# A multi-query attention and expert kernel: w1's turned blocks by way of DRAM, the last batch's rows turned by VectorE, Wq loaded between rows B and C

## The chip, the cores and the metric

One core of a Trainium2 chip runs the whole program. The metric is the device time of one execution in microseconds (us), the median over the runs. Beside it there is one profiled execution, taken by the hardware profiler, with a record of each instruction and its waits.

## The reference

For 8 batches of 1024 rows of 128 numbers, all in float32 (cut to what matters):

```python
xn = layernorm(x)                                  # x: (8, 1024, 128)
Q = einsum('bnd,hdk->bhnk', xn, proj_q)            # 8 query heads
K = einsum('bmd,dk->bmk', xn, proj_k)              # one key head
V = einsum('bmd,dv->bmv', xn, proj_v)              # one value head
weights = softmax(einsum('bhnk,bmk->bhnm', Q, K), axis=-1)
O = einsum('bhnm,bmv->bhnv', weights, V)
Y = einsum('bhnv,hdv->bnd', O, proj_o)
mid = einsum('amh,ehn->aemn', xn, w1)              # w1: (8, 128, 512)
ffn = einsum('aemn,enh->amh', mid, w2)             # w2: (8, 512, 128)
return x + Y + ffn
```

The expert part has no nonlinearity, so it is one 128 x 128 matrix, the sum over experts of w1 times w2. In the same way query and key weights are multiplied together per head (`wqk`), and value and output weights (`wvo`).

## The kernel before

**Tiles.** The unit of work is a score tile i: 128 queries of one head u = i // 8 against the 1024 keys of its batch; there are 8 batches x 8 heads x 8 = 512 tiles (`NS`). For each tile TensorE makes the scores in one of two PSUM slots of 1024 columns (`logits`, tile `pl`: 8 matmuls), VectorE takes the row maxima (`nmax`), ScalarE the exponents and their sums (`e`, two buffers) and scales them by the reciprocal (`divide`). VectorE turns the weights in 32 x 32 blocks (`weights_t`, tile `turned`, two buffers of four tiles each), and after every fourth tile SP issues 16 DMAs of 128 KB, each from 32 partitions to 32, that bring the blocks to their places (`move_blocks`, into `g0` for the first half of a head, `g1` for the second). GpSimd forms sums and differences of halves of these (`sum_early`, `sums_late`: 4.56 us each), and TensorE multiplies them with combinations of the values (`product`) with seven products instead of eight, into four PSUM banks `acc0` to `acc3` that are kept for a whole batch. These products run 12 tiles (`LAG`) behind the scores.

**Order.** The schedule is written by hand: each engine does its instructions in the order of the program, and the loop `for i in range(NS)` at the end of the kernel states it. A DMA that SP issues waits in SP's order for what it reads, and holds all behind it. The first tiles carry, beside the scores, a list `early[i]` of weight preparations. `bank(name)` gives these the four banks `acc0` to `acc3` in turn, before the products need them.

**The start.** The rows of batch 0 (`x_0`) come in four pieces of two chunks each, called A to D here, 128 KB each, on SP's queue; `wk` and Wq (`wq`: head 0 first, then the other seven heads, 448 KB) come on ScalarE's queue, then wv, wo, w1 (2 MB) and w2 on SP's. VectorE makes moments and normalized rows of each pair of chunks (`stats_pair`, `norm_pair`), TensorE transposes them (`xn_t_pair`). `keep_clock` multiplies zeros, so that TensorE is not idle. `wq_part` transposes Wq's heads through a bank and ScalarE copies them out; `wqk_product` multiplies them with the key weights.

**w1 and w2.** The product wants w1 with its middle dimension on the partitions. `turn_w1(k)`, in tiles 0 to 3, has VectorE turn a quarter of w1 in blocks of 32 x 32, into `w1_turned`; in tile 3, after `load_rows(1)` (rows of batch 1, 512 KB), `move_w1` moves the blocks back into the buffer `w1s` with 16 DMAs of 128 KB, 32 partitions to 32. `ffn_weights(k)` multiplies with w2, 32 matmuls in each of tiles 8 to 11, into the bank `pwf` (`acc3`), and the result `wfT`, which lies in the buffer of the value weights `s_v`, is transposed to `wf` in tile 12.

**Rows of later batches.** For batch b > 0 the rows are loaded ahead, normalized by GpSimd, turned by VectorE in blocks (`turn_rows`, tile `xnt`) and moved by 16 DMAs of 32 KB in runs of 1 KB, four each at four tiles (`move_rows`), into `xnT`. The columns of `xnT` are then in the order of these blocks. The last batch is different: it needs the natural order, and `xn_t` has TensorE transpose its eight chunks into a score slot, from which ScalarE copies them.

Of the kernel before, what the change touches and what calls it, by code (L numbers as in the profile page):

```python
# [17 lines left out]
def kernel(  # L18
# [42 lines left out]
    nc = tc.nc  # L61
# [24 lines left out]
    rows = ctx.enter_context(tc.tile_pool(name="rows", bufs=3))  # L86
    work = ctx.enter_context(tc.tile_pool(name="work", bufs=2))
    small = ctx.enter_context(tc.tile_pool(name="small", bufs=4))
    ps_sc = ctx.enter_context(tc.tile_pool(name="ps_sc", bufs=2, space=PSUM))
    ps_acc = ctx.enter_context(tc.tile_pool(name="ps_acc", bufs=1, space=PSUM))  # L90

# [3 lines left out]
    def slot(name):  # L95
        return ps_sc.tile([P, S], F32, tag="sc", name=name)
# [7 lines left out]

    def bank(name):

        banks[0] = (banks[0] + 1) % (3 if pwf else 4)
        return ps_acc.tile([P, GS], F32, tag=f"acc{banks[0]}", name=name)


# [50 lines left out]
    x_0 = late.tile([P, NB, D], F32, tag="x", name="x_0")  # L161
    for i in range(GN):
        nc.sync.dma_start(x_0[:, ts(i, 2)], chunked(x[0])[:, ts(i, 2)])
    nc.scalar.dma_start(wq[:, 1:], proj_q[1:].rearrange("h d k -> d h k"))
    nc.sync.dma_start(wv, proj_v)
    nc.sync.dma_start(wo, proj_o.rearrange("h d v -> d h v"))
    nc.sync.dma_start(w1s.rearrange("p (e n) -> p e n", e=NE), w1.rearrange("e h n -> h e n"))
# [21 lines left out]
    wqk = const.tile([P, H, P], F32, tag="wqk", name="wqk")  # L189
    wvo = const.tile([P, H, P], F32, tag="wvo", name="wvo")  # L190
    wf = const.tile([P, P], F32, tag="wf", name="wf")
    spread = const.tile([P, 3 * HP], F32, tag="spread", name="spread")
    moments = const.tile([P, B, NB, 2], F32, tag="moments", name="moments")
    rstd = const.tile([P, B, NB], F32, tag="rstd", name="rstd")
# [3 lines left out]
    def transposed(dst, srcs, name, copy):  # L198

        pt = blocks(bank(name))  # L200
        for c, src in enumerate(srcs):
            nc.tensor.transpose(pt[:, c, :], src, ident)  # L202
        copy(dst, pt[:, : len(srcs), :])
# [12 lines left out]
        both_halves(pt, wvT, woT[:, ts(g, GN), :])  # L216
        nc.scalar.copy(wvo[:, ts(g, GN), :], blocks(pt))

    wfT = s_v[:, :P]
    w1T = w1s.rearrange("p (r i a) -> p r i a", r=NQ, a=Q)  # L220

    def turn_w1(k):

        i = ts(k, NB)
        nc.vector.transpose(
            w1_turned.rearrange("p (k i a) -> p i k a", k=NQ, a=Q)[:, i],
            w1s.rearrange("p (i k q) -> p i k q", k=NQ, q=Q)[:, i],
        )

    def move_w1():  # L230
        n = NE * NFC * Q
        for r in range(NQ):
            for k in range(NQ):
                nc.sync.dma_start(w1s[ts(k, Q), ts(r, n)], w1_turned[ts(r, Q), ts(k, n)])  # L234

    def ffn_weights(k):
        if k == 0:
            pwf.append(ps_acc.tile([P, GS], F32, tag="acc3", name="pwf"))
        n = NE * NFC
        for i in range(8 * k, 8 * k + 8):  # L240
            w2_i = w2s[2 * i // n][:, i % (n // 2)]
            both_halves(pwf[0][:, :P], w2_i, w1T[:, :, i, :], i == 0, i == n - 1)
        if k == 3:
            nc.scalar.copy(wfT, pwf.pop()[:, :P])
# [30 lines left out]
            xns.pop(b).rearrange("p c (k q) -> p c k q", q=Q),  # L275
        )

    def move_quarters(dst, src, r):

        n = S // NQ  # L280
        for k in range(NQ):
            nc.sync.dma_start(dst[ts(k, Q), ts(r, n)], src[ts(r, Q), ts(k, n)])

    def move_rows(b, r):

        if r == 0:
            xnTs[b] = batch.tile([P, S], F32, tag="xnT", name=f"xnT_{b}")
        move_quarters(xnTs[b], turned_rows[b], r)
        if r == NQ - 1:
            del turned_rows[b]  # L290

    def xn_t(b):
        xnTs[b] = batch.tile([P, S], F32, tag="xnT", name=f"xnT_{b}")
        pt = slot(f"pxn_{b}")
        for c in range(NB):
            nc.tensor.transpose(pt[:, ts(c, P)], xns[b][:, c, :], ident)
        nc.scalar.copy(xnTs[b], pt)

    def xn_t_pair(k, copy):

# [352 lines left out]
    def one(t):  # L653
        return t.rearrange("p (c x) -> p c x", c=1)

    def wq_part(first, last):
        transposed(
            wqT[:, first:last], [wq[:, h] for h in range(first, last)], f"pwq_{first}", nc.scalar.copy
        )

    def wo_part(g):
        heads = range(g * GN, (g + 1) * GN)
# [10 lines left out]
    def norm_pair(k):  # L673
        normalize(0, x_0, nc.vector, (2 * k, 2 * k + 1))

    def stats_pair(k):
# [15 lines left out]
    xn_t_pair(1, nc.scalar.copy)  # L692
    stats_pair(2)
    queries(0, 0, P)
    keep_clock(P)
    stats_pair(3)
    logits_half(0, 0)
    norm_pair(2)
    xn_t_pair(2, nc.scalar.copy)
    norm_pair(3)  # L700
    wq_part(1, 4)
    xn_t_pair(3, nc.vector.tensor_copy)
    logits_half(0, 1)
    wq_part(4, 8)
    queries(0, P, GS)
    exponents(0)

    early = {
        0: [lambda: wqk_product(1, 3), lambda: queries(0, GS, S)],
        1: [  # L710
            lambda: wqk_product(4, 4),
            lambda: queries(1, 0, GS),
# [42 lines left out]
    for i in range(NS):  # L755
        m = i % GN
        if i > 0:
            logits(i)
        for task in early.get(i, ()):
            task()  # L760
        if 0 <= i - 1 < NS - GN:
            weights_t(i - 1)
        divide(i)
        if i < 4:
            turn_w1(i)
        if i == 3:
            load_rows(1)
            move_w1()


        v, n = divmod(i - LAG, NB)
        if n == 6 and v + 1 >= 0:
            sum_early(v + 1)


        if i >= LAG:
            run((PAIRS if i < NS - GN else LAST_PAIRS)[m] + (n == 0 and v % H == H // 2 + 1) * 2)
            if n == 0:
                sums_late(v, nc.gpsimd)
        if i % NB == 0 and i > 0 and i // NB + 1 < B * H:  # L780
            queries(i // NB + 1)
        if i % NB == GN and i >= LAG:
            s, r = divmod(i + 20, 32)
            if s < 2 * B:
                values(s, r // NB)


        if i == 8:
            load_x(0)
        if i == NS // B:  # L790
# [79 lines left out]
```

## Time and profile before

| | us |
|---|---|
| median of 4 runs | 1924.18 |
| lowest and highest | 1923.86 and 1924.26 |
| the profiled execution, whole | 1924.22 |
| its span, first to last instruction | 1922.3 |

| engine | busy us of the span |
|---|---|
| TensorE (PE) | 1911.9 |
| GpSimd (POOL) | 1406.1 |
| VectorE (DVE) | 1396.5 |
| ScalarE (ACT) | 1357.8 |

TensorE's granted clock is 1.000 of full speed over the whole span. DMAs move 295 MB, 154 GB/s on average. In the lists below, PE is TensorE, PEld its weight loads, SPq a DMA issue by SP, and L103 is line 103 of the kernel; L103 is a helper that all products in two halves share, so they are told apart by the tile that they write: `pl` scores, `pq` queries, `pv` values, `pwqk`, `pwvo` and `pwf` weights. A matmul's length includes its way through the array, so successive groups overlap a little; groups of eight start every 1.72 us where nothing waits. A window line gives the window, its length, the busy time of PE, PEld, DVE, ACT and POOL with the number of instructions, the clock, the busy share of the DMA engines and what they moved in GB/s.

### The profile page before, as it was taken

Reading aid. Unit: us, or ns where it says so; the run is one execution under the profiler, and the core shown is the slowest. Engines: PE = TensorE matmul, PEld = TensorE weight load, DVE = VectorE, ACT = ScalarE, POOL = GpSimd, SP = SyncE. Lnnn points to the kernel's source line nnn. Section 1 sums busy time; section 2 is a strip of 40 time slices with the busy share of each in tenths; the row PEclk is TensorE's granted clock in tenths of the full one; section 3 lists DMA queues with packets and bytes.
Section 4 is the critical chain, followed back from the end, with each engine's and each line's share of the span. In section 5 each row is a group of like instructions: output and inputs, shape, how many; then the busy total and the mean of one; then the engine's idle time right before and its main releaser. Section 6 shows DMA issues by size and latency. Waiting matters only on the chain.

```text
span 1922.3 us, 26881 instructions
## 1 busy us (share of the span) xinstructions
PE 1911.9 (99%) x9037; PEld 664.4 (35%) x9037; DVE 1396.5 (73%) x1774; ACT 1357.8 (71%) x1829; POOL 1406.1 (73%) x593
## 2 busy tenths in 40 slices
PE   9999999999999999999999999999999999999998
PEld 4444443333333333333333333333333333333333
DVE  6767778767786777777777777776777776777775
ACT  7677777777777777777777777777777766777764
POOL 2787777788776886777967778768787676677764
PEclk9999999999999999999999999999999999999999
DMA  7776667666766766677667676676766667567673
GB/s 206 173 158 149 141 154 155 152 161 154 158 146 151 172 149 148 151 159 166 142 153 158 150 173 143 149 155 148 183 137 141 145 155 172 132 140 158 153 163 90
DMA packets 138074, 295.08 MB, mean 154 GB/s; under 512 B 36816, under 2 KB 70352, under 8 KB 137936
## 3 DMA queue, kind: packets, MB, share of 16 engines
q1 hardware_dynamic: 136192, 292.50, 67.8%
q8 instruction: 73, 1.20, 0.3%
q10 hardware_dynamic: 1744, 0.85, 0.2%
q14 instruction: 65, 0.53, 0.1%
HBM read 13.76 MB, written 4.19 MB: 9 GB/s over the span
## 4 chain that ended last, share of the span: by engine, by line
PE 96%; SPq 1%; ACT 1%; DVE 1%; DMA 0%; issue 0%; DVEq 0%
PE pl L103 45%; PE acc L460 39%; PE pq L103 6%; PE pv L103 5%; PE acc L493 1%; SPq L415 1%; SPq L234 0%; DVE nmax L359 0%; ACT e L367 0%; DMA x<-in_L_attn_x_dram 0%; ACT e L377 0%; DVE turned L399 0%; ACT scratch_vf L367 0%; PE pe L388 0%; ACT scratch_vf L377 0%
## 5 line engine op out<-in xcount | busy, mean ns | idle before, releaser
L103 PE MATMUL pl<-xnT,qT 128*64 128x512 f32 x4096 | 968.7, 593 | 2.7 <-ACT qT L317 1.5
L359 DVE TENSOR_REDUCE nmax<-pl 128x1 f32<-128x1024 f32 x512 | 625.8, 1222 | 413.7 <-PE pl L103 413.0
L460 PE MATMUL acc<-g,vf 128*64 128x512 f32 x2560 | 852.9, 592 | 0.2 <-PE pwf_t L202 0.2
L367 ACT ACTIVATE e<-pl,nmax 128x1024 f32<-128x1024 f32 x508 | 565.7, 1114 | 399.4 <-DVE nmax L359 399.4
L377 ACT ACTIVATE e<-e,rinv 128x1024 f32<-128x1024 f32 x508 | 583.6, 1149 | 118.7 <-DVE rinv L376 118.6
L399 DVE STREAM_TRANSPOSE turned<-e 128x1024 f32<-128x1024 f32 x508 | 628.3, 1237 | 14.8 <-DMA g<-turned 4.0
L103 PEld LDWEIGHTS pl<-xnT,qT 128*64 128x64 f32 x4096 | 299.5, 137 | 580.0 <-issue 529.3
L460 PE MATMUL acc<-f,vf 128*64 128x512 f32 x1016 | 487.0, 592 | 0.0
L435 POOL TENSOR_TENSOR g<-g,g 128x2048 f32<-128x2048 f32 x63 | 287.0, 4556 | 270.7 <-DMA g<-turned 145.1
L460 PEld LDWEIGHTS acc<-g,vf 128*64 128x64 f32 x2560 | 253.0, 137 | 504.6 <-issue 499.3
L430 POOL TENSOR_TENSOR f<-g 128x2048 f32<-128x2048 f32 x63 | 287.0, 4556 | 175.2 <-PE acc L460 89.8
L438 POOL TENSOR_TENSOR f<-g,g 128x2048 f32<-128x2048 f32 x63 | 287.4, 4562 | 4.9
L436 POOL TENSOR_TENSOR g<-f,g 128x2048 f32<-128x2048 f32 x63 | 287.0, 4555 | 0.0
L460 PEld LDWEIGHTS acc<-f,vf 128*64 128x64 f32 x1016 | 139.2, 137 | 0.0
L103 PE MATMUL pq<-xnT,wqk 128*64 128x512 f32 (+1 forms) x516 | 121.6, 589 | 0.0
L103 PE MATMUL pv<-wvo,xnT 128*64 128x512 f32 x512 | 120.9, 592 | 0.0
L376 DVE RECIPROCAL rinv<-sums 128x1 f32<-128x1 f32 x512 | 83.7, 164 | 48.8 <-ACT scratch_vf L367 4.3
L367 ACT ACTIVATION_READ_ACCUMULATOR e<-pl,nmax 128x1 f32 x508 | 97.2, 191 | 0.0
L337 POOL TENSOR_TENSOR vf<-vf 128x256 f32<-128x256 f32 x64 | 46.8, 732 | 28.5 <-ACT vf L336 28.5
L317 ACT COPY qT<-pq 128x1024 f32<-128x1024 f32 (+2 forms) x67 | 64.0, 955 | 0.2 <-PE pq L103 0.2
L103 PEld LDWEIGHTS pv<-wvo,xnT 128*64 128x64 f32 x512 | 37.7, 137 | 72.2 <-issue 68.5
L103 PEld LDWEIGHTS pq<-xnT,wqk 128*64 128x64 f32 x516 | 37.8, 137 | 70.3 <-issue 69.7
(111 smaller groups left out, 543.1 us busy)
## 6 DMA issues: line engine op xcount, KB each, us to landing
g<-turned SPq DMA_DIRECT2D x2032, 128.0 KB, 2.4
xn<-in_L_attn_x_dram SPq DMA_DIRECT2D x7, 512.0 KB, 4.7
out<-yt SPq DMA_DIRECT2D x112, 32.0 KB, 1.9
xnT<-xnt SPq DMA_DIRECT2D x96, 32.0 KB, 1.9
x<-in_L_attn_x_dram SPq DMA_DIRECT2D x6, 512.0 KB, 4.3
out_dram<-x SPq DMA_DIRECT2D x6, 512.0 KB, 5.3
scratch_g<-in_L_ffn_w_dram SPq DMA_DIRECT2D x1, 2048.0 KB, 11.4
scratch_g<-scratch_vf SPq DMA_DIRECT2D x16, 128.0 KB, 2.4
```

The costliest lines, as they stand in the source:

```text
L103: nc.tensor.matmul(dst[r], lhsT=lhsT[:, r], rhs=rhs, start=start, stop=stop)
L317: copy(qTs[u][:, first:last], pq[:, :n])
L359: nc.vector.reduce_max(nmax, pl, AX.X, negate=True)
L367: nc.scalar.activation(es[i], pl, AF.Exp, bias=nmax, accum_out=sums[i])
L376: nc.vector.reciprocal(rinv, sums.pop(i))
L377: nc.scalar.mul(es[i], es[i], rinv)
L399: nc.vector.transpose(turned[k].rearrange("p k c t q -> p c k t q")[:, :, :, j, :], es.pop(i).rearrange("p (c k q) -> p c k q", k=NQ, q=Q),)
L430: nc.gpsimd.tensor_add(f1s[u], key_half(g0s[u], 0), key_half(g0s[u], 1))
L435: engine.tensor_sub(x1, y1, x1)
L436: engine.tensor_sub(x2, f1s[u], y1)
L438: engine.tensor_sub(f4s[u], y2, x2)
L460: nc.tensor.matmul(accs[b, acc][ts(half, HP)], lhsT=vfs[u // GN][:, u % GN, f, c, :], rhs=w[:, :, c, :], start=(h == 0 and c == first), st ...
```

## The change

Four parts:

- The seven heads of Wq are loaded on SP's queue, between the pieces B and C of the rows. Three of them are transposed where an idle matmul stood, ahead of the first scores, the other four ahead of the second half of tile 0's scores; the copies are separate steps, and the product of heads 1 to 3 comes before the queries of tile 0's second part.
- Each turned quarter of w1 is stored in a DRAM tile as soon as VectorE has turned it; in tile 3, after the rows of batch 1, four loads of 512 KB, each to 32 partitions, bring all of it back into `w1s` in its new order.
- `ffn_weights` moves from tiles 8 to 11 to tiles 9 to 12 and from `acc3` to `acc2`; its result gets a tile of its own, and its transposition moves from tile 12 to tile 14.
- The last batch's rows are turned by VectorE and moved like those of the others, with a destination that restores the natural order: 16 DMAs of 32 KB in pieces of 128 bytes. `xn_t` is gone.

```diff
--- before.py
+++ after.py
@@ -86,6 +86,7 @@
+    dram = ctx.enter_context(tc.tile_pool(name="dram", bufs=1, space=bass.MemoryType.DRAM))
@@ -104,7 +105,8 @@
 
     def bank(name):
 
-        banks[0] = (banks[0] + 1) % (3 if pwf else 4)
+        assert not pwf
+        banks[0] = (banks[0] + 1) % 4
         return ps_acc.tile([P, GS], F32, tag=f"acc{banks[0]}", name=name)
 
 
@@ -161,7 +163,8 @@
     x_0 = late.tile([P, NB, D], F32, tag="x", name="x_0")
     for i in range(GN):
         nc.sync.dma_start(x_0[:, ts(i, 2)], chunked(x[0])[:, ts(i, 2)])
-    nc.scalar.dma_start(wq[:, 1:], proj_q[1:].rearrange("h d k -> d h k"))
+        if i == 1:
+            nc.sync.dma_start(wq[:, 1:], proj_q[1:].rearrange("h d k -> d h k"))
     nc.sync.dma_start(wv, proj_v)
     nc.sync.dma_start(wo, proj_o.rearrange("h d v -> d h v"))
     nc.sync.dma_start(w1s.rearrange("p (e n) -> p e n", e=NE), w1.rearrange("e h n -> h e n"))
@@ -189,6 +192,7 @@
     wqk = const.tile([P, H, P], F32, tag="wqk", name="wqk")
     wvo = const.tile([P, H, P], F32, tag="wvo", name="wvo")
     wf = const.tile([P, P], F32, tag="wf", name="wf")
+    wfT = const.tile([P, P], F32, tag="wfT", name="wfT")
     spread = const.tile([P, 3 * HP], F32, tag="spread", name="spread")
     moments = const.tile([P, B, NB, 2], F32, tag="moments", name="moments")
     rstd = const.tile([P, B, NB], F32, tag="rstd", name="rstd")
@@ -216,26 +220,28 @@
         both_halves(pt, wvT, woT[:, ts(g, GN), :])
         nc.scalar.copy(wvo[:, ts(g, GN), :], blocks(pt))
 
-    wfT = s_v[:, :P]
     w1T = w1s.rearrange("p (r i a) -> p r i a", r=NQ, a=Q)
 
+    w1_way = dram.tile([P, NQ, NE * NFC, Q], F32, tag="w1", name="w1_turned")
+
     def turn_w1(k):
 
         i = ts(k, NB)
+        turned_i = w1_turned.rearrange("p (k i a) -> p k i a", k=NQ, a=Q)[:, :, i]
         nc.vector.transpose(
-            w1_turned.rearrange("p (k i a) -> p i k a", k=NQ, a=Q)[:, i],
+            turned_i.rearrange("p k i a -> p i k a"),
             w1s.rearrange("p (i k q) -> p i k q", k=NQ, q=Q)[:, i],
         )
-
-    def move_w1():
-        n = NE * NFC * Q
-        for r in range(NQ):
-            for k in range(NQ):
-                nc.sync.dma_start(w1s[ts(k, Q), ts(r, n)], w1_turned[ts(r, Q), ts(k, n)])
+        nc.sync.dma_start(w1_way[:, :, i], turned_i)
+
+    def load_w1_turned():
+        for k in range(NQ):
+            src = w1_way.rearrange("(r q) k i a -> k q r (i a)", q=Q)[k]
+            nc.sync.dma_start(w1s[ts(k, Q)].rearrange("q (r n) -> q r n", r=NQ), src)
 
     def ffn_weights(k):
         if k == 0:
-            pwf.append(ps_acc.tile([P, GS], F32, tag="acc3", name="pwf"))
+            pwf.append(ps_acc.tile([P, GS], F32, tag="acc2", name="pwf"))
         n = NE * NFC
         for i in range(8 * k, 8 * k + 8):
             w2_i = w2s[2 * i // n][:, i % (n // 2)]
@@ -275,26 +281,21 @@
             xns.pop(b).rearrange("p c (k q) -> p c k q", q=Q),
         )
 
-    def move_quarters(dst, src, r):
-
+    def move_rows(b, r):
+
+
+        if r == 0:
+            xnTs[b] = batch.tile([P, S], F32, tag="xnT", name=f"xnT_{b}")
         n = S // NQ
         for k in range(NQ):
-            nc.sync.dma_start(dst[ts(k, Q), ts(r, n)], src[ts(r, Q), ts(k, n)])
-
-    def move_rows(b, r):
-
-        if r == 0:
-            xnTs[b] = batch.tile([P, S], F32, tag="xnT", name=f"xnT_{b}")
-        move_quarters(xnTs[b], turned_rows[b], r)
+            dst, src = xnTs[b][ts(k, Q)], turned_rows[b][ts(r, Q), ts(k, n)]
+            if b < B - 1:
+                nc.sync.dma_start(dst[:, ts(r, n)], src)
+            else:
+                dst = dst.rearrange("p (c r q) -> p r c q", r=NQ, q=Q)[:, r]
+                nc.sync.dma_start(dst, src.rearrange("p (c q) -> p c q", q=Q))
         if r == NQ - 1:
             del turned_rows[b]
-
-    def xn_t(b):
-        xnTs[b] = batch.tile([P, S], F32, tag="xnT", name=f"xnT_{b}")
-        pt = slot(f"pxn_{b}")
-        for c in range(NB):
-            nc.tensor.transpose(pt[:, ts(c, P)], xns[b][:, c, :], ident)
-        nc.scalar.copy(xnTs[b], pt)
 
     def xn_t_pair(k, copy):
 
@@ -653,10 +654,15 @@
     def one(t):
         return t.rearrange("p (c x) -> p c x", c=1)
 
-    def wq_part(first, last):
-        transposed(
-            wqT[:, first:last], [wq[:, h] for h in range(first, last)], f"pwq_{first}", nc.scalar.copy
-        )
+    pwqs = {}
+
+    def turn_wq(first, last):
+        pwqs[first] = blocks(bank(f"pwq_{first}"))
+        for h in range(first, last):
+            nc.tensor.transpose(pwqs[first][:, h - first, :], wq[:, h], ident)
+
+    def copy_wq(first, last):
+        nc.scalar.copy(wqT[:, first:last], pwqs.pop(first)[:, : last - first])
 
     def wo_part(g):
         heads = range(g * GN, (g + 1) * GN)
@@ -692,21 +698,28 @@
     xn_t_pair(1, nc.scalar.copy)
     stats_pair(2)
     queries(0, 0, P)
-    keep_clock(P)
+    turn_wq(1, 4)
     stats_pair(3)
     logits_half(0, 0)
+    copy_wq(1, 4)
     norm_pair(2)
     xn_t_pair(2, nc.scalar.copy)
     norm_pair(3)
-    wq_part(1, 4)
     xn_t_pair(3, nc.vector.tensor_copy)
+    turn_wq(4, 8)
     logits_half(0, 1)
-    wq_part(4, 8)
+    copy_wq(4, 8)
+    wqk_product(1, 3)
     queries(0, P, GS)
     exponents(0)
 
+    def turn_wf():
+        pt = ps_acc.tile([P, P], F32, tag="acc2", name="pwf_t")
+        nc.tensor.transpose(pt, wfT, ident)
+        nc.scalar.copy(wf, pt)
+
     early = {
-        0: [lambda: wqk_product(1, 3), lambda: queries(0, GS, S)],
+        0: [lambda: queries(0, GS, S)],
         1: [
             lambda: wqk_product(4, 4),
             lambda: queries(1, 0, GS),
@@ -719,11 +732,11 @@
         5: [lambda: values(0, 2)],
         6: [lambda: values(0, 3)],
         7: [lambda: wvo_product(1)],
-        8: [lambda: ffn_weights(0)],
-        9: [lambda: ffn_weights(1)],
-        10: [lambda: ffn_weights(2)],
-        11: [lambda: ffn_weights(3)],
-        12: [lambda: transposed(one(wf), [wfT], "pwf_t", nc.scalar.copy)],
+        9: [lambda: ffn_weights(0)],
+        10: [lambda: ffn_weights(1)],
+        11: [lambda: ffn_weights(2)],
+        12: [lambda: ffn_weights(3)],
+        14: [turn_wf],
     }
 
     PAIRS = (2, 2, 1, 2)
@@ -765,7 +778,7 @@
             turn_w1(i)
         if i == 3:
             load_rows(1)
-            move_w1()
+            load_w1_turned()
 
 
         v, n = divmod(i - LAG, NB)
@@ -794,10 +807,7 @@
             if r in ROWS:
                 ROWS[r](b)
             r = i - 20 if b == 1 else i - (b - 1) * H * NB
-            if b == B - 1:
-                if r == 3:
-                    xn_t(b)
-            elif r in (0, 4, 8, 12):
+            if r in (0, 4, 8, 12):
                 if r == 0:
                     turn_rows(b)
                 move_rows(b, r // 4)
```

More of the change, by code (lines that the diff above doesn't have):

```diff
@@ L276, in turn_rows @@
         )
-    def move_quarters(dst, src, r):
-        n = S // NQ
-        for k in range(NQ):
-            nc.sync.dma_start(dst[ts(k, Q), ts(r, n)], src[ts(r, Q), ts(k, n)])
     def move_rows(b, r):
@@ L287, in move_rows @@
             xnTs[b] = batch.tile([P, S], F32, tag="xnT", name=f"xnT_{b}")
-        move_quarters(xnTs[b], turned_rows[b], r)
+        n = S // NQ
+        for k in range(NQ):
+            dst, src = xnTs[b][ts(k, Q)], turned_rows[b][ts(r, Q), ts(k, n)]
[4 more added lines that the diff above has]
+                nc.sync.dma_start(dst, src.rearrange("p (c q) -> p c q", q=Q))
         if r == NQ - 1:
             del turned_rows[b]
-    def xn_t(b):
-        xnTs[b] = batch.tile([P, S], F32, tag="xnT", name=f"xnT_{b}")
-        pt = slot(f"pxn_{b}")
-        for c in range(NB):
-            nc.tensor.transpose(pt[:, ts(c, P)], xns[b][:, c, :], ident)
-        nc.scalar.copy(xnTs[b], pt)
     def xn_t_pair(k, copy):
```

## The prediction

> **What bounds the kernel now.** I read the page first, then the chain of waits, then TensorE's order of time where it idles. The page:
>
> ```profile
> span 1922.3 us, 26881 instructions
> PE 1911.9 (99%) x9037; PEld 664.4 (35%) x9037; DVE 1396.5 (73%) x1774; ACT 1357.8 (71%) x1829; POOL 1406.1 (73%) x593
> PE 96%; SPq 1%; ACT 1%; DVE 1%; DMA 0%; issue 0%; DVEq 0%
> ```
>
> TensorE is the limit; only its own work and its few gaps are worth anything. From 60 us on, the list of waits gives TensorE's matmuls less than 1 us of waiting in 1860. So the gaps to look at are in the first 60 us. TensorE's order of time there (start, length, group, and in brackets the idle time before it and who ended it):
>
> ```profile
> 9.17 1.08 PE L103 MATMUL pl<-xnT,qT 128*64 128x512 f32 x4 [1.51 <-ACT qT L317]
> ...
> 11.77 1.08 PE L103 MATMUL pl<-xnT,qT 128*64 128x512 f32 x4 [0.61 <-DVE xnT L306]
> ...
> 56.58 1.94 PE L103 MATMUL pl<-xnT,qT 128*64 128x512 f32 x8 [0.28 <-ACT e L367]
> 59.30 0.33 PE L202 MATMUL pwf_t<-ident,scratch_vf 128*128 128x128 f32 x1 [0.78 <-ACT scratch_vf L244]
> 59.85 1.94 PE L460 MATMUL acc<-g,vf 128*64 128x512 f32 x8 [0.23 <-PE pwf_t L202]
> ```
>
> Two gaps of the start (1.51 and 0.61 us) and a cluster near 57 us. From 56.30, when the matmuls before it end, to 63.51, when the scores of tile 13 start, 7.2 us pass for three groups of 1.72 us: 2.05 us lost, of which one transposition (0.15) is work. What sets this cluster is in the chain of waits (start, length, what):
>
> ```profile
> 28.55 1.24 DVE scratch_vf L225
> 29.80 0.61 SPq L234
> ...
> 40.02 0.54 SPq L415
> ...
> 50.71 2.18 DMA g<-turned
> 52.89 1.23 DVE turned L399
> ```
>
> VectorE ends the last quarter of w1 at 29.8; SP issues the 16 w1 moves (0.63 us each, 10.1 us), then the 16 moves of block 0 (40.0 to 50.6); the last lands at 52.9. Only then is a `turned` buffer free for VectorE's transposition of tile 8 (L399), which had waited 4.0 us. The exponents of tile 10 end 3.6 us later, and tile 12's scores start at 56.58, 3.7 us behind the landing.
>
> **The start.** Three Wq transpositions take the place of one idle matmul in the 1.51 us gap, four more go into the 0.61 us gap, behind the last row pair. Before, they stood between score groups and took 0.33 us (chain: 10.61) and 0.59 us (12.85). So 0.33 + 0.59 = 0.9 us leave the path. Their copies on ScalarE go into its idle 0.90 and 2.01 us. The product of heads 1 to 3 (0.66 us) only changes places with queries. The price is the loading: the 9.17 wait goes back to rows C (x chunks 4, 5), landing at 7.49, 5.71 us after issue where an x piece has a median of 2.9: 448 KB of Wq from ScalarE's queue shared the engines. Now Wq stands wholly ahead of C in one queue. If Wq had already gone ahead, nothing changes; if C had half the engines, C comes 0.5 us later; if one queue serves it faster, up to 0.8 us earlier (128 KB pieces ahead of it landed in 2.6 to 2.9). I take 0, since C landed close to Wq (about 7.9): Wq, landing some 0.5 us earlier than that, is there for the 1.51 us gap. Lead of TensorE after the start: 0.9 us (0.4 to 1.7).
>
> **w1's round trip.** Removed: 16 issues, 10.1 us of SP. Added: four stores, the first three in a stretch where the DMA share is near zero (24 to 29 us), and four loads of 512 KB. SP's order is now store 4, rows of batch 1, loads (which wait until store 4 has landed), moves of block 0; only those moves are queued behind that wait, and VectorE's tile 8 waits for them. Step by step:
>
> - VectorE ends at 29.8 - 0.9 = 28.9.
> - Store 4, 512 KB to DRAM: stores of this size land in 5.4 us (median, engines two thirds busy); a 128 KB one at the end of the kernel in 1.9 to 2.6, so 512 KB without load at least 2.9 (384 KB more at 386 GB/s). I take 4.4, between the two, because only the rows' 512 KB run beside it: 33.3.
> - First data 1.2 us after an issue (29.80 to 31.0): 34.5.
> - Loads, 2.1 MB. Between 386 GB/s (w1 from DRAM to 128 partitions, 9 to 13 us) and 207 (moves into 32 partitions), that is 5.4 to 10.1 us. Nearest are the x pieces, also DRAM to 32 partitions:
>
> ```profile
> 63.00:63.50 0.50, 0.50 (x6) 0.23 (x4) 0.04 (x1) 0.02 (x1) 0.00 (x0) 1.00 0.82 235
> 63.50:64.00 0.50, 0.50 (x5) 0.17 (x2) 0.00 (x0) 0.45 (x1) 0.01 (x1) 1.00 0.85 249
> ```
>
>  The last two columns are DMA share and GB/s: 235 to 249 at 0.82 to 0.85 of the engines, some 290 at full; I take 270, 7.8 us: 42.3. TensorE's first w1T product now stands one tile later, at 44.7, so it is covered by 1.8 us.
> - Moves of block 0: issued from 35.8, 4 us earlier than before, but now queued on the engines behind the loads. 2.1 MB at 215 GB/s (221 at a share of 1.0) are 9.8 us: 52.1, landed 0.6 later: 52.7, with 48.8 and 56.3 as the ends of all bounds.
>
> So the landing that sets tile 12 moves from 52.9 to 52.7: ten microseconds of issuing turn into waiting for a store and for bytes. And the gap grows: the four w2 products (1.72 us each) start one tile later, so only three instead of four stand ahead of tile 12's scores. TensorE is ready for them at 56.30 - 1.72 - 0.9 = 53.7 and gets them at 52.7 + 3.7 = 56.4. The lead of the start is lost in this gap. What is gained is that `pwf` sits in acc2 and `wfT` in a tile of its own: the 0.78 and 0.23 us waits can't recur, but TensorE's fourth w2 product fills that place, so after tile 12 all runs without a gap: from 56.4 four groups of 1.72 us to 63.3, against 63.51. Net -0.2 us. It can't gain over 0.9 + 1.9 = 2.8, reached at a landing of 50.0; at 56.3 it loses 3.4. The `pwf_t` transposition, now at tile 14, costs 0.15 to 0.33: +0.2.
>
> [...]
>
> **The last batch.**
>
> ```profile
> 1441.69 1.09 PE L296 MATMUL pxn<-ident,xn 128*128 128x128 f32 x8
> ```
>
> Eight transpositions, from 1441.60 to the next group at 1442.72: -1.1 us of TensorE on the path. The copy on ScalarE (0.99) and a score slot go too; neither was waited for. Added: one VectorE transposition (1.23 us, VectorE busy 8.4 of 14 us there) and 16 SP issues, in four groups of 2.5 us. Batches 1 to 6 do the same (in batch 6 at 1206, 1222, 1235 and 1252): GpSimd's L435 then waits some 3.9 us for moves queued behind (1207.99), and TensorE doesn't: GpSimd's sum ends at 1212.5, its first reader is near 1220. In that batch TensorE's groups follow each other at 1.72 us, but for 0.2 us at 1240.5. New are 128-byte pieces, 4096 where those batches have 512 of 1 KB. No row has such pieces. If one costs as 512 bytes do (256 in 0.45 us at 290 GB/s), a group is 1.8 us, below its issuing: nothing. If one costs as 4 KB (0.3 us per engine), a group is 19 us, and four groups lose some 50 us against a slack of 5 to 7. I take nothing: a piece of an eighth of 1 KB lies nearer to the 512-byte row.
>
> [...]
>
> **Sum**, against the profiled execution's own 1924.22 (span 1922.3), which is within 0.04 us of the median 1924.18: -0.2 + 0.2 - 1.1 = -1.1, so 1923.1. That is -0.06%; about 0.2% (3.85 us) is what a measurement of this kernel can tell from no change.
>
> **Rivals.**
> - *Loads at the 128-partition rate.* 5.4 us for 2.1 MB, landing at 50.3, gap nearly gone: -2.6 + 0.2 - 1.1 = -3.5; with C 0.8 us earlier -4.3: 1919.9 to 1921.2. For it: the load reads DRAM in 4 KB runs and doesn't read SBUF, which the moves do. Against: 249 GB/s is the most that 32 partitions show.
> - *The round trip holds the queue* (slower side). Store 5.4 us, loads at 207 GB/s, moves at 207: 28.9 + 5.4 + 1.2 + 10.1 + 10.1 + 0.6 = 56.3. It decides from a landing of 53.8, where the loss (0.9) and `pwf_t` (0.2) eat the 1.1 of the last batch; at its end +2.5, with C 0.5 late +3.0: up to 1927.2.
> - *The 128-byte pieces hold the moves.* Over 5 us per group, it costs 4 us or more: above 1928.
> - *Wq late*, so that its transpositions only move the wait: lead 0 instead of 0.9, and everything after it 0.9 later: 1924.0.
>
> **How the numbers follow.** Forecast (landing within 1.3 us of 52.7, Wq late included): 0.50. Fast loads 0.20, of which 0.08 passes -3.85. Held queue 0.22, of which 0.04 passes +3.85 with terms that I missed. Small pieces 0.08. So faster by over 0.2% 0.08, slower 0.12, within 0.80. Range: 1920.4 (most of the fast loads in) to 1926.8 (most of the held queue in).
>
> **What would show it.** Right: the score groups near 9 and 11 us 0 to 1 us earlier, the second gap gone; landing of `turned` near 52 to 53; a single TensorE gap of 2 to 3 us near 55 and none at `pwf_t`; no `pxn` at 1441 and no TensorE wait in the 50 us behind. Wrong: a landing before 50 or after 55, C later than 8 us, or GpSimd's waits near 1440 followed by TensorE's.

## The result: 3.4 us slower, above the range

| | us |
|---|---|
| before, median of 54 runs | 1924.01 (1923.01 to 1925.36) |
| after, median of 34 runs | 1927.43 (1924.62 to 1930.14) |
| after / before | 1.0017, 95% interval 1.0012 to 1.0021 |
| the profiled execution of after, whole | 1926.85 |

The forecast was 1923.1, its range ended at 1926.8. The profiled execution is 2.63 us longer than that of before (1924.22). The page of after, top lines and the chain's shares by engine:

```profile
span 1924.9 us, 26866 instructions
PE 1912.1 (99%) x9027; PEld 648.6 (34%) x9027; DVE 1398.1 (73%) x1775; ACT 1357.0 (70%) x1828; POOL 1406.7 (73%) x593
PE 92%; DVE 2%; ACT 2%; DMA 2%; SPq 1%; POOL 1%; issue 0%; DVEq 0%; POOLq 0%
```

TensorE is still the limit. That 4% of the chain have gone from it to others is not the loss: most of that lies behind 70 us, where TensorE's list of waits holds 0.7 us in all, as before. What is lost shows in its order of time at the start (columns as before):

```profile
9.02 1.08 PE L104 MATMUL pl<-xnT,qT 128*64 128x512 f32 x4 [1.32 <-ACT qT L318]
...
11.30 1.08 PE L104 MATMUL pl<-xnT,qT 128*64 128x512 f32 x4 [0.17 <-DVE xnT L307]
...
46.21 1.97 PE L104 MATMUL pwf<-scratch_g,scratch_f 128*64 128x128 f32 x32 [0.64 <-DMA scratch_g<-w_turned]
...
53.16 1.95 PE L104 MATMUL pwf<-scratch_g,scratch_f 128*64 128x128 f32 x32
58.37 2.97 PE L104 MATMUL pl<-xnT,qT 128*64 128x512 f32 x8 [3.26 <-ACT e L368]
61.11 2.62 PE L104 MATMUL pwf<-scratch_g,scratch_f 128*64 128x128 f32 x32
63.56 1.89 PE L461 MATMUL acc<-g,vf 128*64 128x512 f32 x8
65.28 1.89 PE L104 MATMUL pv<-wvo,xnT 128*64 128x512 f32 x8
67.00 1.89 PE L104 MATMUL pl<-xnT,qT 128*64 128x512 f32 x8
```

Three things are to be seen. The start is faster: the two gaps have shrunk. Then one gap of 3.26 us stands ahead of tile 12's scores. And the two groups behind it take longer: 2.97 instead of 1.94, 2.62 instead of 1.95, with nothing to wait for. Tile 13's scores start at 67.00; in the order of time of before they stand at

```profile
63.31 1.92 PE L103 MATMUL pl<-xnT,qT 128*64 128x512 f32 x8
```

so they are 3.69 us later. Tile 15's are 4.10 us later (73.42 against 69.32), as the transposition of `wfT` now stands between them. The last batch gives 1.1 back: the scores that followed its eight transpositions start at 1445.68 instead of 1442.72, +2.96. The last 0.3 of the way to 2.63 lie behind the last products.

The gap's origin, in the chain of waits of after (start, length, what):

```profile
28.59 3.65 DMA w_turned<-scratch_vf
...
33.88 12.19 DMA scratch_g<-w_turned
...
46.09 0.51 SPq L416
...
47.91 1.34 SPq L416
...
52.51 2.15 DMA g<-turned
54.66 1.24 DVE turned L400
```

The last move of block 0 lands at 54.66, 1.8 us later than before (52.89). Tile 12's scores start 3.7 us behind it, as before. Before, the chain ran through SP's issues from 29.8 to 50.7; now it runs through one store, the loads, and the moves that SP issued only after the last load (46.07).

The long groups are explained by the windows of after (the clock is the third number from the end):

```profile
33.00:41.00 8.00, 8.00 (x38) 2.44 (x34) 6.21 (x8) 7.56 (x13) 7.08 (x11) 1.00 1.02 211
...
58.00:59.00 1.00, 0.64 (x4) 0.34 (x6) 1.00 (x3) 0.77 (x3) 1.00 (x1) 1.00 0.89 205
59.00:60.00 1.00, 1.00 (x6) 0.24 (x2) 0.91 (x2) 1.00 (x2) 0.20 (x1) 0.57 0.94 209
60.00:61.00 1.00, 1.00 (x4) 0.24 (x2) 1.00 (x2) 0.87 (x2) 0.00 (x0) 0.50 0.62 131
61.00:62.00 1.00, 1.00 (x12) 0.89 (x10) 0.69 (x2) 0.90 (x1) 0.00 (x0) 0.50 0.52 115
62.00:63.00 1.00, 1.00 (x16) 1.00 (x14) 1.00 (x2) 0.61 (x2) 0.00 (x0) 0.73 0.88 197
```

TensorE's granted clock falls to half for some 3.4 us, starting after the gap is over. From 58.37 to tile 13 there are four groups, 6.88 us at 1.72 each; they took 8.63, so the half clock costs 1.75 us. The first window belongs to the loads: 211 GB/s with the DMA engines full (share 1.02).

**The two theories that the experiments had to part.** Theory: the late landing (rate of the loads, and SP held by them) and the half clock that its gap brings, about half of the loss each. Rivals: the half clock only comes along, and the gap alone counts; only the bytes ahead of the moves count, not their order; or another part of the change costs the time.

### The profile page after: what moved, and what is told of

It is laid out like the page before. It is cut to its first block, busy times and chain, and to the rows that moved or that the text cites. A ratio compares the mean times of both kernels' runs of the same rounds, so it can differ in the third digit from the quotient of the medians.

```text
span 1924.9 us, 26866 instructions
## 1 busy us (share of the span) xinstructions
PE 1912.1 (99%) x9027; PEld 648.6 (34%) x9027; DVE 1398.1 (73%) x1775; ACT 1357.0 (70%) x1828; POOL 1406.7 (73%) x593
## 4 chain that ended last, share of the span: by engine, by line
PE 92%; DVE 2%; ACT 2%; DMA 2%; SPq 1%; POOL 1%; issue 0%; DVEq 0%; POOLq 0%
PE pl L104 43%; PE acc L461 38%; PE pq L104 5%; PE pv L104 5%; DVE nmax L360 1%; SPq L416 1%; ACT e L368 1%; PE acc L494 1%; DMA scratch_g<-w_turned 1%; DVE turned L400 1%; DMA g<-turned 0%; ACT e L378 0%; DMA x<-in_L_attn_x_dram 0%; POOL f L439 0%; POOL g L436 0%
## 5 line engine op out<-in xcount | busy, mean ns | idle before, releaser
L104 PEld LDWEIGHTS pl<-xnT,qT 128*64 128x64 f32 x4096 | 292.3, 137 | 591.2 <-issue 535.4
```

What stands on the lines that cost most here:

```text
L104: nc.tensor.matmul(dst[r], lhsT=lhsT[:, r], rhs=rhs, start=start, stop=stop)
```

## Experiments

All have 5 rounds, with runs of before on the same chip (medians 1924.15 to 1924.28). "Gap" is TensorE's wait ahead of tile 12's scores, "landing" that of block 0's last move, read where VectorE's transposition that waited for it starts; both are from the profiled execution.

### The parts alone, on before

**Round trip alone**: before with the four stores and four loads, nothing else; w2 products in tiles 8 to 11 as before.

```diff
+        nc.sync.dma_start(w1_way[:, :, i], turned_i)
...
-            move_w1()
+            load_w1_turned()
```

> The kernel before with w1's round trip alone: four stores and four loads in place of the 16 moves, the w2 products in tiles 8 to 11 and in acc3 as before. Theory: the loads end at about 47.3, 5 us after TensorE wants the first w2 product (42.2), so TensorE idles 5 us there and its clock dips for some 3.4 us; block 0 lands near 55.9 instead of 52.9, with less of a gap ahead of tile 12's scores, and the wait for the result of the w2 products stays: 3 to 6 us slower than before, 1927 to 1930. Rival (the round trip is hidden and the other parts of the change cost the time): 1924.

Measured: 1928.59, ratio 1.0022 (1.0013 to 1.0032), +4.4 us. TensorE's order of time:

```profile
46.17 3.68 PE L104 MATMUL pwf<-scratch_g,scratch_f 128*64 128x128 f32 x32 [4.53 <-DMA scratch_g<-w_turned]
```

and its windows:

```profile
44.00:46.00 2.00, 0.00 (x0) 0.00 (x0) 1.52 (x8) 1.35 (x3) 0.00 (x0) 0.53 1.07 227
46.00:48.00 2.00, 1.82 (x18) 1.86 (x20) 0.00 (x0) 0.00 (x0) 0.00 (x0) 0.50 1.03 229
48.00:50.00 2.00, 2.00 (x20) 1.88 (x18) 0.00 (x0) 0.00 (x0) 0.00 (x0) 0.50 1.05 238
```

Here the first w2 product itself waits 4.53 us for the loads, and the clock is halved again, this time from inside the gap on. The round trip is the loss. In after, where the first product stands a tile later, its wait is only 0.64 us. That this makes the whole loss smaller is not shown: the three parts alone (+4.4, and -1.0 and -0.6 below) sum to +2.8, and after measured +3.4.

**Last batch alone**: before, with `xn_t` replaced by turned rows and 128-byte moves.

```diff
-            if b == B - 1:
-                if r == 3:
-                    xn_t(b)
-            elif r in (0, 4, 8, 12):
+            if r in (0, 4, 8, 12):
```

> The kernel before with the last batch's rows turned by VectorE and moved in 128-byte pieces, and nothing else changed. Theory: eight transpositions of TensorE (1.1 us) leave its path, no wait takes their place: 1923.0 to 1923.1. Rival (the pieces hold the block moves, and TensorE waits near 1440): above 1925.

Measured: 1923.18, ratio 0.9994 (0.9986 to 1.0003): -1.0 us in the medians, as expected, though the interval takes in 1.

**Start alone**: before, with Wq between B and C on SP's queue and the new order of its transpositions.

```diff
-    nc.scalar.dma_start(wq[:, 1:], proj_q[1:].rearrange("h d k -> d h k"))
+        if i == 1:
+            nc.sync.dma_start(wq[:, 1:], proj_q[1:].rearrange("h d k -> d h k"))
```

> The kernel before with the start alone: Wq on SP's queue between rows B and C, its transpositions in the two gaps, the product of heads 1 to 3 ahead of the queries. Theory: TensorE is ahead by 0.9 us (0.33 and 0.59 us of transpositions off its path) when tile 1's scores start (14.7 instead of 15.6), VectorE's last quarter of w1, SP's moves, block 0's landing and all behind it follow by as much, since nothing else sets them: 0.9 us below before, 1923.3. Rival (C lands later behind Wq): the wait ahead of the first scores grows by 0.5 to 1 us and nothing is gained, 1924.2.

Measured: 1923.67, ratio 0.9997 (0.9988 to 1.0005): -0.6, two thirds of what was expected and not told from zero. Tile 1's scores start 1.3 us earlier, but the landing only 0.5 (52.41), and the gap ahead of tile 12 grows from 0.28 to 0.96. A lead of TensorE's is worth what the landing follows of it. SP's first w1 move still starts 1.16 us earlier (28.64 against 29.80). Some 0.7 of that go in block 0's moves, where one issue takes 1.81 us instead of the usual 0.59; before has two that take 0.69 and 1.02.

### Is the half clock a cause?

**Fourth product ahead**: after, with the fourth w2 product in tile 11, so that it fills 1.72 us of the gap and keeps it short.

```diff
-        11: [lambda: ffn_weights(2)],
-        12: [lambda: ffn_weights(3)],
+        11: [lambda: ffn_weights(2), lambda: ffn_weights(3)],
```

> The changed kernel with the fourth w2 product in tile 11, behind the third, instead of tile 12. Theory (late landing and clock): in the changed kernel TensorE idles 3.3 us ahead of tile 12's scores, and the profile then grants it about half the clock for some 3.4 us, which costs 1.75 us (scores 2.97 instead of 1.94, fourth product 2.62 instead of 1.95). With 1.72 us of work moved into the gap, the gap is about 1.6 us, the clock stays at 1.000, and both 1.72 and 1.75 us are gained: about 1924.0, with runs as close to each other as the kernel before's (within 1 us of the median). Rival (only the order counts, the clock belongs to the run): 1.7 us gained, 1925.7, and the clock's dip stays. Rival (time set by the landing, whatever stands ahead): 1927.4.

Measured: 1923.59, ratio 0.9998 (0.9989 to 1.0007), 3.8 us below after. In its order of time the gap is 1.85 us and the group behind it has its normal length:

```profile
57.88 1.94 PE L104 MATMUL pl<-xnT,qT 128*64 128x512 f32 x8 [1.85 <-ACT e L368]
```

One product of 1.72 us, moved by one tile, brings over twice its length. In the two profiles tile 13's scores start 3.92 us earlier (63.08 against 67.00): 1.72 for the product, 1.75 for the clock, and 0.49 because tile 12's scores start that much earlier. Behind them a product has a new wait of 1.33 us, which the list of waits puts down to a DMA of rows, so the profiled execution is only 2.5 us shorter than that of after (1924.33).

**Gap filled**: after, with matmuls of zeros behind the third product. They bring nothing forward; only the clock can gain.

```diff
+    def fill_gap():
+        pgap = ps_acc.tile([P, GS], F32, tag="acc1", name="pgap")
+        for _ in range(4):
+            both_halves(pgap, idle[:, :P], idle)
...
-        11: [lambda: ffn_weights(2)],
+        11: [lambda: ffn_weights(2), fill_gap],
```

> The changed kernel with eight matmuls of zeros (64 columns of weights, 512 of data, 1.72 us in all) behind the third w2 product, in a bank that is free; no useful work is moved. Theory (late landing and clock): tile 12's scores start when they did (58.4), the idle time ahead of them falls from 3.3 to about 1.6 us, the clock stays at 1.000 and 1.75 us are gained: about 1925.6, with a smaller spread. Rival (idle time itself is the loss): nothing is gained, 1927.4.

Measured: 1925.01, ratio 1.0005 (0.9996 to 1.0014), 2.4 us below after. The order of time:

```profile
54.48 3.63 PE L104 MATMUL pgap<-idle 128*64 128x512 f32 x16
...
58.76 1.94 PE L104 MATMUL pl<-xnT,qT 128*64 128x512 f32 x8 [0.65 <-ACT e L368]
```

and a window where after had 0.57:

```profile
59.00:60.00 1.00, 1.00 (x6) 0.29 (x4) 1.00 (x1) 1.00 (x1) 0.61 (x1) 1.00 0.88 201
```

The filler ran twice as many matmuls as meant (x16, 3.63 us), yet it ends at 58.1 and delays nothing: tile 12's scores still wait 0.65 us behind it, and they start 0.39 us later than in after because the landing is 0.40 later (55.06). Still the profiled execution is 1.36 us shorter (1925.49), as 0.39 - 1.75 = -1.36 would have it. Useless work gains what the half clock had cost, so the rival that the gap alone counts is out. That the two profiles agree to the last digit is luck.

The spread of after's runs fits this. Its runs (35 are listed), by the mean granted clock of each: 5 at 1.000 with a median of 1924.8, 20 at 0.999 with 1926.8, 10 at 0.998 with 1928.3. 3.4 us at half clock lower the mean by 1.7/1925 = 0.0009, so to 0.999 (the profile of after); the round trip alone, whose profile lists 0.998, has half clock from 44.1 to 50.9, twice that long. So the gap seems to bring no, one or two such stretches, by the execution. Of the runs without a trace this is inferred, not seen, and the last digit alone is weak: of 27 runs of before, 7 list 0.999 too, and their median (1924.1) is no longer than that of the others (1924.5). In the kernels with gaps of 1.85 and 2.40 us, two of eleven runs each list 0.999 and are 2.1 and 3.3 us longer than the median of the rest, so a shorter gap may now and then bring a half clock as well; no trace shows it.

In the profiles the half clock goes with the length of the gap: those of 1.85 us (fourth product ahead), 1.87 (w1 within SBUF) and 2.40 us (loads to 128 partitions) brought none, those of 3.15 (sixteen loads), 3.26 (after), 4.20 (rows ahead) and 4.53 us (round trip alone) all did. By the windows the clock fell 2.5 to 4.1 us after the idle time had begun, and stayed at half for 3.4 us, or for 6.8 in the round trip alone. What sets these times no run tests.

### What makes the landing late?

**w1 within SBUF**: after, with the 16 moves of before in place of stores and loads.

```diff
-            load_w1_turned()
+            move_w1()
```

> The changed kernel with w1's turned blocks moved by the 16 moves within SBUF as in the kernel before; all else as changed. Theory (the round trip is what lands late): block 0 lands about 51.7 instead of 54.7 (52.9 before, less the lead of 1.2), the gap ahead of tile 12's scores is about 1.7 us, no dip of the clock, tile 13's scores at 62.3, and with the last batch's 0.9 less: 1921.9. Rival (the later w2 products or the Wq order make the gap, the round trip costs nothing): 1926 to 1927.

Measured: 1922.48, ratio 0.9992 (0.9983 to 1.0001), 5 us below after. Landing 51.99, no half clock, and the gap is

```profile
55.69 1.94 PE L104 MATMUL pl<-xnT,qT 128*64 128x512 f32 x8 [1.87 <-ACT e L366]
```

So all of the loss is the round trip's, and the other parts keep some 1.7 us, with an interval that just takes in 1.

**Loads to 128 partitions**: after, with the DRAM tile laid out in the order of the destination. Sixteen stores of 128 KB put each block at its place; four loads of 512 KB each go to 128 partitions.

```diff
-        nc.sync.dma_start(w1_way[:, :, i], turned_i)
+        way = w1_way.rearrange("(k q) r i a -> q k r i a", q=Q)
+        for r in range(NQ):
+            nc.sync.dma_start(way[:, :, r, i], turned_i[ts(r, Q)])
...
-            src = w1_way.rearrange("(r q) k i a -> k q r (i a)", q=Q)[k]
-            nc.sync.dma_start(w1s[ts(k, Q)].rearrange("q (r n) -> q r n", r=NQ), src)
+            dst = w1s.rearrange("p (r i a) -> p r i a", r=NQ, a=Q)
+            nc.sync.dma_start(dst[:, k], w1_way[:, k])
```

> The changed kernel with the DRAM tile laid out in the order of the destination: each quarter is stored by four DMAs of 128 KB from 32 partitions (16 issues in place of 4), and the four loads of 512 KB each fill a quarter of the columns of all 128 partitions, in 4 KB runs. Bytes, number and size of the loads are as in the changed kernel. Theory (loads that fill 32 partitions are what is slow: they hold the DMA engines at 205 GB/s with a share of 1.03, where w1's first load to 128 partitions ran at 386): the loads take some 6 us instead of 11 to 12, block 0 lands at 51.6 although the last store is 1.9 us later, the gap ahead of tile 12's scores is about 1.6 us, no dip of the clock: 1922.0. Rival (a read of what was just written to DRAM is slow, or the queue's depth): landing at 55 or later, 1927 to 1928.

Measured: 1922.38, ratio 0.9994 (0.9985 to 1.0003). Two of its windows:

```profile
33.00:41.00 8.00, 8.00 (x40) 2.50 (x38) 6.21 (x8) 7.56 (x13) 7.09 (x11) 1.00 1.03 324
...
46.00:48.00 2.00, 2.00 (x30) 1.43 (x28) 0.77 (x1) 1.41 (x4) 0.00 (x0) 1.00 0.21 49
```

With full engines 324 GB/s flow where after had 211. Landing 52.87 (expected 51.6), gap 2.40, no half clock. The second line is the rest of the answer: from 46 to 48 the engines are nearly empty, though SP has been at block 0's moves since 33.0 us. The bytes are no longer what they wait for. SP's list of waits in this kernel (who waits, for whom, us in all, times, longest):

```profile
SPq L418 <- DMA scratch_g<-w_turned: 5.3, 4, 2.0
```

and in after:

```profile
SPq L416 <- DMA scratch_g<-w_turned: 7.5, 4, 2.1
```

L416 of after issues block 0's moves, which read nothing of w1. Each still waits until the eighth DMA before it has landed: the program uses eight completion semaphores in turn on this queue (in the trace of after SP's 2305 DMAs signal on eight, 288 or 289 each). With rows and four loads among the eight, four moves go out from 34.4 to 36.4 us, the fourth once the rows have landed, then one for each load that lands, and the rest only from 46.1 on, at 0.6 us each. In after the four loads land at 38.74, 41.14, 43.79 and 46.07, and SP's next issues start at 38.75, 41.16, 43.80 and 46.09. The lists of waits fit this in the other kernels: four waits for the four loads here (5.3 us), five in each of the next two (1.4 and 2.3 us).

One more thing sits in these landings: in each profile one issue of block 0's moves, or two together, takes far longer than the usual 0.59 us. In after it is the line at 47.91 above, 1.34 us; in this kernel's chain of waits it is

```profile
44.94 2.19 SPq L418
```

The empty stretch from 46 to 48 lies in and just behind this issue. The last load had landed before, at 43.7, so the wait for it, which the expectation of the eight wide loads below gives as the reason, is not the whole of it. In after a DMA of instructions (0.02 MB, queue q8 in the DMA view) runs at the same time, for 1.2 us from some 47.7 on; in this kernel the view has one between 30 and 48 us. Whether it is what holds SP was not tested.

**Sixteen loads**: after, each load split in four of 128 KB, still to 32 partitions. Bytes and rate as in after; only the size and number of the loads differ.

```diff
+                for r in range(NQ):
+                    nc.sync.dma_start(dst[:, r], src[:, r])
```

> The changed kernel with each load of 512 KB in four of 128 KB, still to 32 partitions: 16 loads, the same bytes, the same runs. The program waits, before it issues a DMA, until the eighth before it has landed; in the changed kernel SP issued only 8 of block 0's moves between 34.4 and 46, one for each load that landed. Theory A (the rate to 32 partitions, 205 GB/s, sets the loads' end and through it block 0): the loads still end at 44 to 45, the moves follow without a pause, block 0 lands 0.5 to 1 us earlier (about 54), the gap ahead of tile 12's scores is 2.6 us and dips the clock in few runs: 1924.5 to 1925.5. Theory B (eight large DMAs in flight are what holds the moves): block 0 lands about 51.5, no gap to speak of, 1922 or less. Rival C (neither): 1927.4.

Measured: 1925.78, ratio 1.0007 (0.9998 to 1.0016). The window of the loads:

```profile
33.00:41.00 8.00, 8.00 (x38) 2.50 (x36) 6.21 (x9) 7.56 (x13) 7.09 (x11) 1.00 1.02 214
```

So 214 GB/s, nearly as in after. Landing 53.38, 1.3 earlier; SP's waits for loads 1.4 us in all instead of 7.5. But the gap is still over the edge:

```profile
57.08 3.26 PE L104 MATMUL pl<-xnT,qT 128*64 128x512 f32 x8 [3.15 <-ACT e L370]
```

**Eight wide loads**: loads to 128 partitions in eight of 256 KB, so both the rate and the number in flight differ from after.

```diff
-            nc.sync.dma_start(dst[:, k], w1_way[:, k])
+            for i in (slice(0, 16), slice(16, 32)):
+                nc.sync.dma_start(dst[:, r, i], w1_way[:, r, i])
```

> The kernel with loads to 128 partitions (w1's DRAM tile in the order of the destination), with eight loads of 256 KB in place of four of 512 KB. With four loads to 128 partitions the DMA engines were nearly idle from 45.5 to 47.5 (56 GB/s), as SP waited for the last load (landing 43.7) before it could issue on. Theory (both the rate to 32 partitions and the eight DMAs in flight): each load that lands lets one move go, the moves run from about 36 on, block 0 lands near 50 instead of 52.9, and the gap of 2.4 us ahead of tile 12's scores is gone: 1920.0 to 1921.0. Rival (one slow DMA engine sets the last landing, whatever the sizes): landing at 52.5, 1922.4.

Measured: 1922.04, ratio 0.9988 (0.9979 to 0.9996), one us above what was expected. Landing 51.48, gap 0.78; SP waits 2.3 us for loads. Against after's landing of 54.66, the number in flight alone brings 1.3, the rate alone 1.8, both together 3.2. That the parts add up so well is luck, since the one slow issue differs: 0.75 us over the usual 0.59 in after, 0.92 with sixteen loads, 1.60 with four wide ones, 0.90 here. Without it (an estimate) they would be 1.5, 2.6 and 3.3: both count, the rate more.

**Rows ahead**: after, with batch 1's rows loaded in tile 0, so that 512 KB less stand beside the last store and the loads.

```diff
+        if i == 0:
+            load_rows(1)
...
-            load_rows(1)
             load_w1_turned()
```

> The changed kernel with the rows of batch 1 (512 KB) loaded in tile 0, ahead of the first store, where SP issued them before the change; so they don't stand between the last store and the loads. Theory (the DMA engines' bytes set block 0's landing): 512 KB fewer at about 300 GB/s, landing 1.7 us earlier at 53.0, gap 1.6 us, no dip of the clock: about 1924.0. Rival (the wait for the store and SP's issuing set it): landing unchanged, 1927.4; with half of it, and the clock's dip in some runs, about 1925.5.

Measured: 1926.31, ratio 1.0010 (1.0002 to 1.0019), so the theory that bytes alone set the landing missed by 2.3 us. The landing is 54.2, only 0.5 earlier; the gap is even longer, because TensorE had a larger lead in this execution:

```profile
57.90 3.57 PE L104 MATMUL pl<-xnT,qT 128*64 128x512 f32 x8 [4.20 <-ACT e L368]
```

The bytes alone are not enough; the runs above on the number in flight have the other part.

### Better versions

**w1 within SBUF, products in tiles 8 to 11**:

```diff
-        9: [lambda: ffn_weights(0)],
+        8: [lambda: ffn_weights(0)],
...
-        12: [lambda: ffn_weights(3)],
+        11: [lambda: ffn_weights(3)],
```

> The changed kernel with w1 moved within SBUF as before, and the four w2 products in tiles 8 to 11 as before, but into acc2 and with the transposition of their result in tile 14. A candidate for a version better than both. Theory: block 0 lands at 52.0, tile 12's scores start at 55.7, and TensorE is ready for them 1.72 us later than with w1 within SBUF alone, at 55.5, so that 0.2 us of the gap of 1.9 are left: 1.7 us below that kernel's 1922.5, so 1920.8. Rival (the w2 products then wait for the moves of w1, which land about 40.3): the same 1922.5.

Measured: 1921.69, ratio 0.9988 (0.9979 to 0.9997), 0.9 above what was expected: the gap is 0.91, since the landing (52.43) didn't follow the lead, and a wait of 0.4 us for rows at a product is new.

**Eight wide loads, fourth product ahead**:

```diff
-        11: [lambda: ffn_weights(2)],
-        12: [lambda: ffn_weights(3)],
+        11: [lambda: ffn_weights(2), lambda: ffn_weights(3)],
```

> The kernel with eight loads to 128 partitions and, in addition, the fourth w2 product in tile 11. A candidate for a version better than both. Theory: the 0.8 us gap that was left ahead of tile 12's scores is filled, and nothing else moves: 1921.3, 0.7 us below the kernel with eight loads alone (1922.0). Rival (the second block's landing then becomes the bound, as in the changed kernel with the fourth product ahead, where the products of tile 13 waited 1.3 us): no gain, 1922.0.

Measured: 1920.99, ratio 0.9984 (0.9975 to 0.9993): 3.2 us below before and 6.4 below after, the best of all kernels here. Its order of time:

```profile
51.85 3.66 PE L104 MATMUL pwf<-scratch_g,scratch_f 128*64 128x128 f32 x64
55.34 1.89 PE L104 MATMUL pl<-xnT,qT 128*64 128x512 f32 x8
```

Landing 50.17, and no gap ahead of tile 12. With a rate and an order that suit it, the round trip is no longer a loss. That it is worth more than the moves that it replaced is not shown: the best kernel with moves within SBUF is 0.7 us slower, the two intervals overlap, and no run has those moves with this order of products.

## Why the prediction was wrong, step by step

**Right.** The lead of the start: 0.9 forecast, in the profile of after 0.19 + 0.44 from the two gaps and the transpositions gone between the score groups, 1.2 us at tile 1. That it would be lost in the gap ahead of tile 12: yes, but for a new wait of 0.68 us ahead of tile 9's scores, and the run with the start alone shows it in part (1.3 us ahead at tile 1, 0.5 at tile 12). The last batch: -1.1 forecast, -1.0 alone. The 128-byte pieces cost nothing: their 16 DMAs land in 2.0 us (median; in other batches 1.9). No wait at `pwf_t`. The store: 3.65 us against 4.4 taken, inside the bounds. Scores of tile 12 at 3.7 us behind the landing: 3.71.

**Wrong: the rate of the loads.** I took 270 GB/s and got 211 to 214 at a full share of the engines. From the first issue (32.33) to the last landing (46.07) 13.7 us passed, where I had 1.2 + 7.8 = 9.0. At 211 GB/s the loads' own 2.1 MB take 9.9 us, so the rate is 2.1 of the 4.7 us missed; the rest is traffic that I had not put beside the loads, such as the rows of batch 1 (issued at 29.16, 6.0 us to landing) and the first moves. The error was to scale the x pieces' 235 to 249 GB/s by their share of 0.82 to 0.85 and to prefer this to the row at 207, which I had as the lower bound and which lies within 2% of the 211 measured. The 324 GB/s of the four loads to 128 partitions are the counter-test. What holds the loads to 32 partitions at 211 no run shows.

**Wrong: how the moves wait.** "Issued from 35.8 ... queued on the engines behind the loads" was the picture. Four were issued from 34.4 to 36.4; the others waited in SP's order, one for each load that landed, until 46. The trace of before could have warned only weakly: with 128 KB each, its DMAs land (2.4 us in the median) faster than eight are issued (5.1 us at 0.63 each). Rate and order together put the landing at 54.66 instead of 52.7, inside my bounds (48.8 to 56.3) and past the 53.8 from which my rival of the held queue decides. That rival was the right case by its landing and its slow loads, but not by all its terms: its store took 5.4 us where 3.65 were measured, and its moves waited on the engines, not in SP's order.

**Missed: the clock.** "From 56.4 four groups of 1.72 us" was wrong twice: from 58.37, and with 8.63 us for the four instead of 6.88. I counted gaps by their length alone. The sum also has a slip: it sets starts from the order of time against 63.51 for tile 13, which is from the chain of waits; in the order of time it is 63.31, so -0.2 should have read 0.0, and the forecast 1923.3. The sum, mended: 0.0 up to tile 13, + 2.0 for the landing, + 1.75 for the clock = +3.75; measured +3.69. Behind that the `pwf_t` transposition cost 0.4 (0.2 forecast) and the last batch gave 1.1, as forecast; 0.3 behind the last products stay unexplained. Priced without the clock, the held queue would have stood at 1923.3 + 2.0 = 1925.3, inside the range. The upper end of the fast loads' rival, 1921.2, follows from no term either: its sum of -3.5 gives 1920.7.

**Also wrong, without effect.** TensorE's first w1T product was to be covered by 1.8 us; it waited 0.64. That only took time out of the gap that followed.

**Still open.** Why the last of the four wide loads landed at 43.7 although 324 GB/s would have brought its bytes by 41; why one of SP's issues in block 0 takes up to 2.2 us, which takes lead away from the landing; and what sets how often and how long the clock is halved.

## What to carry to other kernels

On TensorE, busy for 99% of the span, a gap had two prices here: its length, and, in the four profiles with a gap of 3.15 us or more, a half clock, worth 1.75 us in after; those with gaps of 2.40 us or less had none. By these numbers a change that lengthens a gap from 2 to 3.3 us costs over twice what it seems (an estimate: 1.3 + 1.75), and work that breaks the gap, even useless work, took the second price away (1.36 us in the profile with the gap filled). When many small DMAs become a few large ones ahead of others in a queue, count how many may be in flight and not only the bytes: in after four of the small ones behind were issued one per landing, from 38.75 to 46.09 us. And spread a destination over all partitions before trusting a rate: here the same bytes went at 211 GB/s to 32 of them, at 324 to 128.

## What was not expected of the hardware

- The half clock set in 2.5 us (round trip alone) to 4.1 us (rows ahead) after the beginning of the idle time, even when work had already begun again: in after at some 59.1 us, 0.8 us into the next group. It lasted 3.4 us in three profiles (after, rows ahead, sixteen loads) and 6.8 in the round trip alone, in whose windows the waits went on for 2 us more after the fall.
- DMAs to the four quarters of the partitions, one after the other with full engines, did not add up: four loads to 32 partitions each had 211 GB/s together, sixteen had 214.
- Pieces of 128 bytes within SBUF cost little more than pieces of 1 KB here: in the medians 2.0 against 1.9 us to landing for 32 KB, 0.62 against 0.59 us of SP for each.
